# A 3x3 convolution by four outputs from six products down a column, in place of two outputs from four products along a row

## The chip, the cores and the metric

The kernel runs on one core of a Trainium2 chip. The metric is device microseconds of one launch. In the profile PE is TensorE's matmuls, PEld its weight loads, DVE is VectorE, ACT is ScalarE, POOL is GpSimd, and SP is the engine that issues most DMAs. PSUM is the memory into which matmuls write, SBUF the memory that everything else works in, with 128 partitions each.

## What is computed

32 images of 128 channels and 64 x 64 pixels, float32. Each goes through a group norm, a convolution whose weights are mixed for each image, a windowed attention and a scan over its tokens. The part that the change touches is the convolution:

```python
def _L0_conv_ref(x, kernels, fc_w, fc_b):
    pooled = x.mean(axis=(2, 3))
    coeffs = jax.nn.sigmoid(pooled @ fc_w.T + fc_b)
    coeffs = jax.nn.softmax(coeffs, axis=1)
    dyn_k = jnp.einsum('bk,klmij->blmij', coeffs, kernels)
    # one 3x3 convolution for each image, 128 channels in and out, stride 1, padding 1
    ...
x = x + _L0_conv_ref(_gn(x), L0_conv_kernels, L0_conv_fc_w, L0_conv_fc_b)
t = _to_tokens(x)
t = t + _L1_attn_ref(_ln_t(t), ...)
t = t + _L1_ffn_ref(_ln_t(t), L1_ffn_W, L1_ffn_V, L1_ffn_gamma, L1_ffn_beta)
x = _from_tokens(t, x)
```

There are four kernels of 3 x 3 taps to mix, and `_gn` is a group norm with 32 groups of 4 channels. The attention works on windows of 144 tokens with 4 heads of 4 dimensions. The last layer is a scan over the 4096 tokens of an image.

## The kernel before

Channels lie on the partitions. `images()` does everything up to the scan's input, image by image; `by_runs()` (lines 1615 to 1689) then does the scan in runs of 32 tokens with a warm-up of 20. Between them stands only the scan's batch norm.

**Jobs.** The work of an image is cut into generators: `load`, `conv`, `project`, `feed`, `attend`, `divide` (two) and `tail`. They are all put into one list with a place in an order (lines 1139 to 1144): an image's number plus an offset for its stage, `load` at -2.5, `conv` at 0. `conv` also has its first sort key set, so that it comes last of all. A generator yields what its next step needs: an engine, a PSUM tag, the tiles it reads and writes. The loop at lines 1145 to 1162 asks `Clock`, a model of the engines kept while the program is built, when each could go on. It takes the first in the order that could start before the model's TensorE is free, or else the earliest. What a generator issues between two yields goes out as one block. All of this is fixed when the program is built: on the chip each engine runs its own instructions in that order, and waits on semaphores where data or a buffer is not ready. The `Clock` wrapper issues every instruction from line 173, so that the profile gives L173 for nearly everything in `images()`.

**The convolution before.** It uses a minimal filtering scheme along a row: two neighbouring outputs from four products. At the start (lines 364 to 377) the raw taps of the four kernels are loaded, each row's three taps are turned into four (`g4`), and the result is stored to `k_d` in device memory. `load(b)` fetches the image into one of two frames `xs`, with a border of one pixel (66 columns a row), takes its statistics by `bn_stats`, gets the group mean `gm`, writes it into the border, and works out the four coefficients `co`. It then loads `k_d` in eight pieces `kx` (two buffers, 128 x 768) and mixes them into `wb` (lines 581 to 592).

`conv(b)` goes over four blocks of 16 rows. `transform(i)` (line 607) makes the four inputs `ut` of a block, 18 rows of 32 each: three subtractions on POOL and one operation on DVE. Each of the four products is three matmuls of 512 columns, one for each of the kernel's three rows, summed in one PSUM tile `nm`. There are three such tiles, used by all stages. DVE then adds the product to the even or odd columns of the frame, or to both, so the residual is there already.

**Buffers that other stages use.** `places` (line 422) are five SBUF buffers of 1056 elements. `place()` gives one out, and `spare` lists the free ones. `deviations` uses them for squares and statistics. `spread` uses up to three at once for what it loads from device memory: rows of statistics (`r_d`), spread over the partitions, and pieces of the saved image (`x_d`). The attention's score tile `sc` is one PSUM tile of four banks, and POOL makes its masked queries `qe`.

## Time and profile before

| what | value |
|---|---|
| median of three runs | 5544.47 us (5532.93 to 5547.58) |
| the profiled execution's own span | 5544.0 us |
| mean granted TensorE clock | 0.933 of full speed |
| convolution matmuls, records | 3072 of 43571 |
| first and last convolution matmul start | 91.6 and 4661.5 us |
| DMA traffic | 866.15 MB, mean 156 GB/s |
| kx loads | 256 of 384 KB |
| place loads from r_d and x_d | 512 of 512 KB, 128 of 528 KB |

The profile gives for each engine its busy time and its share of the span. A float32 matmul shows as two records, and records overlap, as matmuls are pipelined. "Idle before" is the time for which an engine stood still ahead of a group's instructions, with the instruction that it waited for. The chain is followed back from the last instruction to what released each step, so its shares say who set the end.

The span in 40 slices shows the stages: a start of about two slices, a steady middle, a thin end of `images()` (slices 35 to 37), and the scan. In each string a digit is the busy share in tenths:

```
PE   3898888979989889898898988998988988749995
DVE  5656765666766667676676676666676665448995
ACT  0344333444444344444444444444444444427884
POOL 1331312222322222222222222222222322105774
PEclk9998999989999999999999999999999999869997
```

### The profile page before, as it was taken

The numbers are of one execution on the slowest core, as the hardware profiler recorded it, in microseconds if no ns is written. First come the engines' busy times: TensorE is split into PE (matmuls) and PEld (weight loads), VectorE is DVE, ScalarE is ACT, GpSimd is POOL, SyncE is SP. The second block draws the span as 40 slices with busy tenths as digits, with TensorE's granted clock in tenths as the row PEclk, the third lists the DMA queues.
The fourth block names the chain that finished last, engine by engine and source line by source line (L and its number), as shares of the span: only waits on it lengthen the run. The fifth ranks groups of instructions, "written<-read, shape, count | busy, mean of one in ns | idle before, by whom it ended". The sixth has DMA issues, their size and how long they took to land.

```text
span 5544.0 us, 106009 instructions
## 1 busy us (share of the span) xinstructions
PE 4768.8 (86%) x43571; PEld 2315.6 (42%) x43571; DVE 3648.5 (66%) x5335; ACT 2453.1 (44%) x3852; POOL 1569.2 (28%) x1625
## 2 busy tenths in 40 slices
PE   3898888979989889898898988998988988749995
PEld 1444434444444444444444444444444444314552
DVE  5656765666766667676676666676666765448995
ACT  0344333444444344444444444444444444427884
POOL 1331312222322222222222222222222322105774
PEclk9998999989999999999999999999999999869997
DMA  4515454453445454454454544445545553454997
GB/s 117 153 63 184 129 163 134 141 168 125 154 149 175 138 159 148 144 163 149 142 170 148 164 155 146 160 158 158 158 143 155 159 160 130 136 213 138 269 279 150
DMA packets 456801, 866.15 MB, mean 156 GB/s; under 512 B 297312, under 2 KB 307824, under 8 KB 423536
## 3 DMA queue, kind: packets, MB, share of 16 engines
q1 hardware_dynamic: 447600, 792.12, 44.7%
q0 software_dynamic: 8704, 67.11, 6.0%
q8 instruction: 348, 5.70, 0.4%
q14 instruction: 149, 1.22, 0.1%
HBM read 575.10 MB, written 275.78 MB: 153 GB/s over the span
## 4 chain that ended last, share of the span: by engine, by line
PE 47%; DVE 21%; DMA 14%; ACT 7%; issue 4%; SPq 3%; POOL 2%; DVEq 0%; ACTq 0%; POOLq 0%
PE nm L173 30%; PE sc L173 10%; DVE zt L173 6%; PE av L173 5%; DMA place<-r_d 4%; DVE v L1665 4%; DMA kx<-k_d 3%; ACT ex L173 3%; SPq L173 3%; DMA av<-cd 2%; DVE v L1659 2%; ACT place L173 2%; DVE place L173 2%; DVE frames L173 2%; DVE wb L173 1%
## 5 line engine op out<-in xcount | busy, mean ns | idle before, releaser
L173 ACT ACTIVATE ex<-sc 128x1152 f32<-128x1152 f32 x896 | 1011.6, 1129 | 1303.0 <-PE sc L173 1299.5
L173 PE MATMUL nm<-ut,wb 128*128 128x512 f32 x3072 | 1566.2, 633 | 16.8 <-DVE wb L173 15.6
L173 POOL TENSOR_TENSOR qe<-qs,mqk 128x576 f32<-128x576 f32 x448 | 586.8, 1315 | 1364.1 <-PE sc L173 1332.8
L173 PE MATMUL sc<-qe,ks 32*128 32x288 f32 x7168 | 724.2, 474 | 252.3 <-ACT ext L173 96.8
L173 PEld LDWEIGHTS nm<-ut,wb 128*128 128x128 f32 x3072 | 535.0, 194 | 617.6 <-issue 591.3
L173 POOL TENSOR_TENSOR ut<-frames 128x576 f32<-128x576 f32 x384 | 529.7, 1409 | 865.1 <-PE nm L173 835.8
L173 PE MATMUL av<-ex,VE 128*32 128x144 f32 x14336 | 654.7, 302 | 22.3 <-DVE av L173 21.8
L173 DVE TENSOR_TENSOR frames<-frames,nm 128x512 f32<-128x512 f32 (+1 forms) x640 | 495.1, 791 | 243.3 <-PE nm L173 236.1
L173 PEld LDWEIGHTS sc<-qe,ks 32*128 32x128 f32 x7168 | 296.9, 191 | 807.7 <-issue 270.4
L173 PEld LDWEIGHTS av<-ex,VE 128*32 128x32 f32 x14336 | 372.8, 112 | 354.4 <-issue 263.0
L173 DVE TENSOR_TENSOR zt<-zt,place 128x1024 f32<-128x1024 f32 x256 | 329.2, 1286 | 134.6 <-DMA place<-r_d 109.9
L173 DVE SCALAR_TENSOR_TENSOR wb<-kx,co,wb 128x768 f32<-128x768 f32 x192 | 231.6, 1206 | 217.6 <-DMA kx<-k_d 215.9
L1664 PE MATMUL v<-yw,fVT 128*128 128x256 f32 x1024 | 327.0, 442 | 43.3 <-ACT yw L1668 42.1
L173 ACT ACTIVATE place<-zt 128x1024 f32<-128x1024 f32 x256 | 263.9, 1052 | 189.3 <-DVE zt L173 166.1
L173 PE MATMUL nm<-av,spr 24*32 24x384 f32 (+1 forms) x1280 | 193.2, 600 | 149.9 <-DMA av<-cd 149.7
L173 DVE TENSOR_TENSOR place<-place 128x256 f32<-128x256 f32 x416 | 217.3, 522 | 150.8 <-ACT place L173 141.3
L1669 POOL COPY zr<-yw 128x256 f32<-128x256 f32 x416 | 257.7, 688 | 128.6 <-ACT yw L1668 128.6
L1668 ACT ACTIVATE yw<-v,shf 128x256 f32<-128x256 f32 x512 | 241.6, 473 | 109.2 <-DVE v L1665 74.5
L1665 DVE SCALAR_TENSOR_TENSOR v<-zr,scl,v 128x256 f32<-128x256 f32 x416 | 254.9, 655 | 43.7 <-PE v L1664 43.7
L173 PE MATMUL nm<-place,avg 128*32 128x256 f32 x3072 | 243.1, 396 | 39.4 <-ACT place L173 38.5
L173 ACT COPY zt<-nm 128x512 f32<-128x512 f32 x256 | 148.6, 586 | 264.5 <-PE nm L173 262.2
L173 DVE TENSOR_TENSOR av<-av,nm 128x384 f32<-128x384 f32 (+1 forms) x160 | 89.7, 570 | 260.6 <-PE nm L173 258.2
(191 smaller groups left out, 6006.0 us busy)
## 6 DMA issues: line engine op xcount, KB each, us to landing
place<-r_d SPq DMA_DIRECT2D x512, 512.0 KB
kx<-k_d SPq DMA_DIRECT2D x256, 384.0 KB
x_d<-frames SPq DMA_DIRECT2D x32, 2112.0 KB
place<-x_d SPq DMA_DIRECT2D x128, 528.0 KB
frames<-in_x_dram SPq DMA_DIRECT2D x128, 512.0 KB
out_dram<-zt SPq DMA_DIRECT2D x64, 1024.0 KB
z_d<-zt SPq DMA_DIRECT2D x64, 1024.0 KB
zr<-z_d SPq DMA_DIRECT2D x26, 2048.0 KB
```

The source lines that it names most:

```text
L173: got = f(*args, **kw)
L1659: nc.vector.scalar_tensor_tensor(ps, z, scl, ps, ALU.mult, ALU.add)
L1664: nc.tensor.matmul(ps, fVT, yw[1 - r % 2], start=True, stop=True)
L1665: nc.vector.scalar_tensor_tensor(ps, zt[:, :, :, r], scl, ps, ALU.mult, ALU.add)
L1668: nc.scalar.activation(yw[r % 2], ps, AF.Sigmoid, bias=shf)
L1669: nc.gpsimd.tensor_copy(zt[:, :, :, r], yw[r % 2])
```

## The change

The convolution is done down a column instead: four outputs from six products. `conv` goes over two halves of 32 rows. A half has eight groups of four rows, and each product is three matmuls (one for each of the kernel's three columns) on 8 x 64 = 512 columns. That is 36 matmuls of nm for an image where there were 48.

The tap transform at the start and `k_d` are gone. `load` loads the raw taps of a kernel (128 x 1152) into a place buffer, two ahead, and mixes the four into `h`, whose middle tap gets 1/6 of the identity added: products are multiplied by 6 at the end, and so the residual comes with the convolution. A place buffer grows to 1152 elements. A new job `taps(b)` makes the tap combinations for four of the products (`ws`), three operations on POOL and three on DVE, with waits for the products of the image before that still read them. A new job `waves(b)` makes the six inputs of each half in nine buffers `us` of 8 x 66 elements: seven operations on DVE and five on POOL for each half.

The evacuation of a half is: two products copied from PSUM by ScalarE (`t`), the others combined by ten DVE operations, which write the frame's rows anew. `conv` waits for its waves (`done["wave", ...]`), and writes only when the raw rows have been read (`done["raw", ...]`, `done["edge", ...]`).

```diff
-    k_d = dram.tile([NK, P, 4, 3, P], F32, name="k_d")
...
+    id6 = const.tile([P, P], F32, name="id6")
+    nc.vector.tensor_scalar_mul(id6, ident, 1.0 / 6.0)
...
-    QT, NPL, NF, NZ = T // 4, 5, 2, 3
+    QT, NPL, NF, NZ, NU = T // 4, 5, 2, 3, 9
...
-            with tc.tile_pool(name="gk", bufs=2) as gk:
-                for k in range(NK):
-                    g3 = gk.tile([P, 3, 3, P], F32, name="g3")
-                    nc.sync.dma_start(
-                        g3.rearrange("p i j l -> p (i j) l"), conv_k[:, k].rearrange("m i j l -> m (i j) l")
-                    )
-                    g4 = gk.tile([P, 4, 3, P], F32, name="g4")
-                    nc.vector.tensor_copy(g4[:, 0], g3[:, :, 0])
-                    nc.vector.tensor_copy(g4[:, 3], g3[:, :, 2])
-                    nc.vector.tensor_add(g4[:, 1], g3[:, :, 0], g3[:, :, 2])
-                    nc.vector.tensor_sub(g4[:, 2], g4[:, 1], g3[:, :, 1])
-                    nc.vector.tensor_add(g4[:, 1], g4[:, 1], g3[:, :, 1])
-                    nc.vector.tensor_scalar_mul(g4[:, 1:3], g4[:, 1:3], 0.5)
-                    nc.sync.dma_start(k_d[k], g4)
...
-            places = [kept([P, 16 * (W + 2)], f"place{i}") for i in range(NPL)]
+            places = [kept([P, 9 * P], f"place{i}") for i in range(NPL)]
...
-                ks4 = []
-                def kernel(n):
-                    ks4.append(two.tile([P, 6, P], F32, name="kx"))
-                    nc.sync.dma_start(
-                        ks4[n], k_d[n % NK, :, 2 * (n // NK) : 2 * (n // NK) + 2].rearrange("p j i l -> p (j i) l")
-                    )
-                for k in range(2):
-                    kernel(k)
...
+                gm6 = sml.tile([P, 1], F32, name="gm6")
+                nc.vector.tensor_scalar_mul(gm6, gm, 6.0)
...
+                done["mean", b] = gm, gm6
...
+                taps = []
+
+                def kernel():
+                    w = yield from place("SP", ())
+                    nc.sync.dma_start(w, conv_k[:, len(taps)].rearrange("m i j l -> m (i j l)"))
+                    taps.append(w)
+
+                for k in range(2):
+                    yield from kernel()
                 yield "PE", "nm", (cv,)
                 gv_ps = nm_tile()
                 nc.tensor.matmul(gv_ps[:, 0:1], grp, cv, start=True, stop=True)
...
+                nc.vector.tensor_scalar_mul(gr, gr, 1.0 / 6.0)
...
-                wb = two.tile([P, 12, P], F32, name="wb")
-                for n in range(2 * NK):
-                    if 0 < n < 2 * NK - 1:
-                        yield "SP", "kx", ()
-                        kernel(n + 1)
-                    yield "DVE", None, (co, ks4[n])
-                    k, w = n % NK, wb[:, 6 * (n // NK) : 6 * (n // NK) + 6]
+                h = two.tile([P, 9 * P], F32, name="h")
+                for k in range(NK):
+                    yield "DVE", None, (co, taps[k]), (h,)
                     if k == 0:
-                        nc.vector.tensor_scalar_mul(w, ks4[n], co[:, 0:1])
+                        nc.vector.tensor_scalar_mul(h, taps[k], co[:, 0:1])
                     else:
-                        nc.vector.scalar_tensor_tensor(w, ks4[n], co[:, k : k + 1], w, ALU.mult, ALU.add)
-                done["load", b] = wb, gm2
+                        nc.vector.scalar_tensor_tensor(h, taps[k], co[:, k : k + 1], h, ALU.mult, ALU.add)
+                    spare.append(taps[k])
+                    if k + 2 < NK:
+                        yield from kernel()
+                nc.vector.tensor_add(h[:, 4 * P : 5 * P], h[:, 4 * P : 5 * P], id6)
+                done["load", b] = h
+            ws = [kept([P, 3 * P], f"w{k}") for k in range(4)]
+            def taps(b):
+                while ("load", b) not in done or (b and gone.get(("conv", b - 1), 0) < 8):
+                    yield
+                h = done["load", b]
+                h0, h1, h2 = (h[:, 3 * P * i : 3 * P * (i + 1)] for i in range(3))
+                yield "POOL", None, (h,), (ws[0], ws[1])
+                nc.gpsimd.tensor_add(ws[1], h0, h2)
+                nc.gpsimd.tensor_add(ws[0], ws[1], h1)
+                nc.gpsimd.tensor_sub(ws[1], ws[1], h1)
+                done["taps", b, 0] = h0, ws[0], ws[1]
+                while b and gone.get(("conv", b - 1), 0) < 12:
+                    yield
+                yield "DVE", None, (h,), (ws[2], ws[3])
+                nc.vector.scalar_tensor_tensor(ws[3], h0, 0.25, h2, ALU.mult, ALU.add)
+                nc.vector.scalar_tensor_tensor(ws[2], h1, 0.5, ws[3], ALU.mult, ALU.add)
+                nc.vector.scalar_tensor_tensor(ws[3], h1, -0.5, ws[3], ALU.mult, ALU.add)
+                done["taps", b, 1] = ws[2], ws[3], h2
+            us = [kept([P, 8, W + 2], f"u{k}") for k in range(NU)]
+            def waves(b):
+                while ("mean", b) not in done or (b and ("waves", b - 1) not in done):
+                    yield
+                gx = xs[b % NF]
+                gm, gm6 = done["mean", b]
+                def new(eng, aps):
+                    while not us:
+                        yield
+                    yield eng, None, aps, (us[0],)
+                    while not us:
+                        yield
+                    return us.pop(0)
+                for i in range(2):
+                    d = [gx[:, 32 * i + k : 32 * i + k + 29 : 4, :] for k in range(6)]
+                    f = yield from new("POOL", (gx,))
+                    nc.gpsimd.tensor_sub(f, d[0], d[2])
+                    done["edge", b, i] = True
+                    u2 = yield from new("DVE", (gx,))
+                    nc.vector.scalar_tensor_tensor(u2, d[2], 4.0, d[4], ALU.mult, ALU.subtract)
+                    u3 = yield from new("DVE", (gx,))
+                    nc.vector.scalar_tensor_tensor(u3, d[1], 4.0, d[3], ALU.mult, ALU.subtract)
+                    u1 = yield from new("DVE", (gx,))
+                    nc.vector.scalar_tensor_tensor(u1, u2, gm6, u3, ALU.subtract, ALU.add)
+                    nc.gpsimd.tensor_sub(u2, u2, u3)
+                    done["wave", b, i, 1], done["wave", b, i, 2] = u1, u2
+                    c = yield from new("POOL", (gx,))
+                    nc.gpsimd.tensor_sub(c, d[4], d[2])
+                    nc.vector.scalar_tensor_tensor(f, c, 0.25, f, ALU.mult, ALU.add)
+                    done["wave", b, i, 0] = f
+                    e = yield from new("POOL", (gx,))
+                    nc.gpsimd.tensor_sub(e, d[3], d[1])
+                    g = yield from new("POOL", (gx,))
+                    nc.gpsimd.tensor_sub(g, d[5], d[3])
+                    done["raw", b, i] = True
+                    nc.vector.scalar_tensor_tensor(g, e, -4.0, g, ALU.mult, ALU.add)
+                    done["wave", b, i, 5] = g
+                    nc.vector.scalar_tensor_tensor(u3, e, 2.0, c, ALU.mult, ALU.add)
+                    nc.vector.scalar_tensor_tensor(c, e, -2.0, c, ALU.mult, ALU.add)
+                    done["wave", b, i, 3], done["wave", b, i, 4] = u3, c
+                    us.append(e)
+                done["waves", b] = True
             def conv(b):
-                while ("load", b) not in done or (b and ("conv", b - 1) not in done):
+                while ("taps", b, 0) not in done or (b and ("conv", b - 1) not in done):
                     yield
                 gx = xs[b % NF]
-                def transform(i):
...
-                ut = transform(0)
-                for i in range(4):
-                    nxt = transform(i + 1) if i < 3 else None
-                    xi = rows(gx, 16 * i, 16)
-                    xe, xo = xi[:, :, 0::2], xi[:, :, 1::2]
-                    for k in (0, 3, 1, 2):
-                        yield "PE", "nm", (wb, ut[:, k])
+                gm, gm6 = done["mean", b]
+                for i in range(2):
+                    y = rows(gx, 32 * i, 32).rearrange("p (t j) w -> p t j w", j=4)
+                    y = [y[:, :, j] for j in range(4)]
+                    for n, k in enumerate((1, 2, 0, 5, 3, 4)):
+                        while ("wave", b, i, k) not in done or (k in (5, 3) and ("taps", b, 1) not in done):
+                            yield
+                        u = done["wave", b, i, k]
+                        if k in (0, 1, 2):
+                            w = done["taps", b, 0][k]
+                        else:
+                            w = done["taps", b, 1][k - 3]
+                        yield "PE", "nm", (w, u)
                         ps = nm_tile()
-                        for di in range(3):
+                        for dj in range(3):
                             nc.tensor.matmul(
-                                ps, wb[:, 3 * k + di], ut[:, k, di : di + 16], start=(di == 0), stop=(di == 2)
+                                ps, w[:, P * dj : P * (dj + 1)], u[:, :, dj : dj + W], start=(dj == 0), stop=(dj == 2)
                             )
-                            if di < 2:
+                            if dj < 2:
                                 yield "PE", None, ()
-                        m = ps.rearrange("p (h w) -> p h w", w=W // 2)
-                        if k == 0:
-                            nc.vector.tensor_add(xe, xe, m)
-                        elif k == 3:
-                            nc.vector.tensor_add(xo, xo, m)
-                        elif k == 1:
-                            x2 = xi.rearrange("p h (w o) -> p h w o", o=2)
-                            nc.vector.tensor_add(
-                                x2,
-                                x2,
-                                m.rearrange("p h (w o) -> p h w o", o=1).to_broadcast([P, 16, W // 2, 2]),
-                            )
+                        us.append(u)
+                        gone["conv", b] = 6 * i + n + 1
+                        m = lines(ps)
+                        if k in (1, 3):
+                            t = one.tile([P, BLK], F32, name="tm")
+                            tl = lines(t)
+                            if k == 1:
+                                nc.scalar.activation(t, ps, AF.Identity, bias=gm)
+                            else:
+                                nc.scalar.copy(t, ps)
+                            continue
+                        while ("raw", b, i) not in done or (i == 0 and ("edge", b, 1) not in done):
+                            yield
+                        if k == 2:
+                            nc.vector.tensor_add(y[2], tl, m)
+                            nc.vector.tensor_sub(y[1], tl, m)
+                        elif k == 0:
+                            nc.vector.scalar_tensor_tensor(y[0], m, 6.0, y[2], ALU.mult, ALU.add)
+                        elif k == 5:
+                            nc.vector.scalar_tensor_tensor(y[3], m, 6.0, y[1], ALU.mult, ALU.add)
                         else:
-                            nc.vector.tensor_add(xe, xe, m)
-                            nc.vector.tensor_sub(xo, xo, m)
-                    ut = nxt
+                            nc.vector.tensor_sub(tl, tl, m)
+                            nc.vector.scalar_tensor_tensor(m, m, 2.0, tl, ALU.mult, ALU.add)
+                            nc.vector.tensor_add(y[0], y[0], m)
+                            nc.vector.scalar_tensor_tensor(y[2], m, 4.0, y[2], ALU.mult, ALU.add)
+                            nc.vector.scalar_tensor_tensor(y[1], tl, 2.0, y[1], ALU.mult, ALU.add)
+                            nc.vector.scalar_tensor_tensor(y[3], tl, 8.0, y[3], ALU.mult, ALU.add)
                 done["conv", b] = gx
...
-                    (tail(b), divide(b, 0), divide(b, 1), attend(b), project(b), load(b), conv(b), feed(b))
+                    (tail(b), divide(b, 0), divide(b, 1), attend(b), project(b), load(b), conv(b), feed(b), taps(b), waves(b))
-                    jobs.append([stage == 6, b + (-0.05, -0.15, 0.6, 1.65, -1.25, -2.5, 0, -0.9)[stage], b, g, None])
+                    at = b + (-0.05, -0.15, 0.6, 1.65, -1.25, -2.5, 0, -0.9, -2.4, -2.3)[stage]
+                    jobs.append([stage == 6, at, b, g, None])

```

## What is predicted

> **What bounds the kernel now.** I read the page first (shares, slices, chain, costliest groups), then the groups with shapes kept apart, then the waits, then one tile at a time, then windows and the timeline.
>
> ```profile
> PE 4768.8 (86%) x43571; PEld 2315.6 (42%) x43571; DVE 3648.5 (66%) x5335; ACT 2453.1 (44%) x3852; POOL 1569.2 (28%) x1625
> ...
> PE 47%; DVE 21%; DMA 14%; ACT 7%; issue 4%; SPq 3%; POOL 2%; DVEq 0%; ACTq 0%; POOLq 0%
> PE nm L173 30%; PE sc L173 10%; DVE zt L173 6%; PE av L173 5%; DMA place<-r_d 4%; DVE v L1665 4%; DMA kx<-k_d 3%; ACT ex L173 3%; SPq L173 3%; DMA av<-cd 2%; DVE v L1659 2%; ACT place L173 2%; DVE place L173 2%; DVE frames L173 2%; DVE wb L173 1%
> ...
> L173 PE MATMUL nm<-ut,wb 128*128 128x512 f32 x3072 | 1566.2, 633 | 16.8 <-DVE wb L173 15.6
> ```
>
> TensorE is busiest, the convolution (nm<-ut,wb) is its largest group, and it hardly waits: 16.8 us idle in front of it. But TensorE makes up only 47% of the chain, so a microsecond taken from it is not surely a microsecond gained. In 500 us windows from 500 to 4500 us TensorE is busy 434 to 454, VectorE 314 to 346. The first convolution matmul starts at 91.6 us and the last at 4661.5: 4570/32 = 143 us an image.
>
> **What goes from TensorE.** Four column blocks of 4 products of 3 matmuls (48 an image) become 2 halves of 6 products of 3 (36), all 128x128 on 512 columns. Each shows as two records (3072 = 32 x 48 x 2). The read pattern changes from 512 contiguous elements to 8 rows of 64 at a pitch of 66; nm<-frames,avg reads rows at that pitch at 391 ns against 396 and 413 for contiguous sources, so I charge nothing. Undisturbed speed:
>
> ```profile
> 2121.16 14.86 PE L173 MATMUL nm<-ut,wb 128*128 128x512 f32 x34
> ```
>
> 14.86/34 = 0.437 us a record; 1566.2/3072 = 0.510 with slow-clock stretches and pipeline ends in it. 12 x 2 x 32 = 768 records: 336 or 392 us. If only chain time counts (47% of 86%, a factor 0.55), 336 gives 185. I take 336, because the convolution comes last in the job order and fills whatever is open: bounds 185 and 392.
>
> **What goes at the start.** Four loads of the raw taps, 28 VectorE operations of about 0.55 us (15 us) and four stores to k_d precede the first image's mean (its copy gm runs at 58.2 us, though mv was done at 27.7); POOL's first setup memset waits 50.1 us for k_d<-g. The setup's small SP issues remain. I take 25 us, bounds 0 and 40.
>
> **VectorE, by image.** The rows:
>
> ```profile
> L173 DVE SCALAR_TENSOR_TENSOR ut<-frames,gm x128: 804/1697/1826, 100.4 to 4617.0; 128x576 f32<-128x576 f32 x128
> ...
> L173 DVE SCALAR_TENSOR_TENSOR wb<-kx,co,wb x192: 999/1019/2033, 81.6 to 4540.8; 128x768 f32<-128x768 f32 x192
> ...
> L173 POOL TENSOR_TENSOR ut<-frames x384: 1136/1166/2837, 59.4 to 4616.8; 128x576 f32<-128x576 f32 x192
> ```
>
> (minimum/median/maximum ns). The ut operation on VectorE, issued beside POOL's, takes 804 ns at least and 1697 in the median: it loses about one POOL operation.
>
> Evacuation: before 495.1/32 = 15.5 us (the frames group). After, per half: 4 tensor-tensor from PSUM at 0.685, 4 scalar-tensor-tensor with PSUM at 0.722 (812 ns for 576, times 512/576), 2 from SBUF at 0.99 (between 0.715 and 1.27, scaled from ut's 804 and mean 1427): 7.6, so 15.2. Saves 0.3.
>
> Waves: 14 of 528 elements, 0.737 to 1.308 (ut's minimum and mean, scaled): 10.3 to 18.3, where 180.1/32 = 5.6 stood. I take the upper, since POOL again works on the same image beside it: +12.7 (low +4.7).
>
> Mixing: before (231.6 + 42.8)/32 = 8.6. After one scaling (669 x 1.5 = 1.0), three accumulations (1206 x 1.5 = 1.8) and 0.3 for the identity: 6.7. Saves 1.9. The three operations for ws are new: 3 x 1206/2 = 1.8.
>
> Sum +12.3 us an image (low +4.3), 394 us busy, 73% in all. VectorE is on the chain with 21% for 66% busy, a factor 0.32: +126 us (low 44).
>
> **A rule against it.** The Trainium skill ("SBUF — State Buffer", section "SBUF: two separate sides") says VectorE and GpSimd share a port pair, locked for a whole instruction, by a VectorE operation with two SBUF inputs against a GpSimd one that reads SBUF, and that the loser blocks fully. That speaks against the change, which has 17 such VectorE and 13 GpSimd operations for each image; the ut row above agrees with it. A sum by the rule, each of the 14 waves losing a whole POOL median of 1.166, would be an estimated 14 x (0.737 + 1.166) = 26.6 us in place of 18.3, some 85 us more after the chain's factor.
>
> **ScalarE and POOL.** ScalarE gets 4 copies of 512 from PSUM (zt<-nm, 586 ns): 2.3 us an image, times 7/44, 12 us in all. POOL had 12 x 1.409 = 16.9; it gets 10 x 1.409 x 528/576 and 3 of 384 elements at 0.893 (the kt group): 15.6. Two transforms are issued at once before, six POOL operations (8.68 us at 2184.93 in the timeline) with the attention's qe queued behind; now each waits its own turn. Nothing is taken for it.
>
> **New waits.** In each half VectorE's f waits for POOL's u2 and c, and g for e and its own subtraction: four in-order waits an image of up to 2 x 1.166 = 2.3 us, 9.3 in all. Behind them on VectorE stand the evacuations of nm's three PSUM tiles, for which TensorE waits next. Steps of other jobs can be put in between, so I take half of 9.3 x 0.32 x 32 = 95, that is 48 (bounds 0 and, all of it exposed, 298).
>
> **DMAs and SP's queue.** Eight kx loads of 384 KB (3.07 MB) become four of 576 KB (2.3 MB), issued by SP among the same place and frame loads.
>
> ```profile
> DVE wb L173 <- DMA kx<-k_d: 232.6, 115, 9.3
> ...
> DVE zt L173 <- DMA place<-r_d: 183.7, 77, 8.0
> ```
>
> kx loads are 3% of the chain, 166 us. By count half would go (83), by bytes a quarter (42). But the taps now live in two of the five place buffers, from before the coefficients until they are mixed, and a load waits for a free one behind deviations and spread. I take 20 gained; the bounds are 83 gained and the loss in rival E.
>
> **Sum.** -336 - 25 + 126 + 12 + 48 - 20 = -195 from a span of 5544.0 us (the median is 5544.47, so the two agree): **about 5350 us**. With the high ends of the costs (TensorE 185, start 0, stalls 298, DMA 0) it is 5544 - 185 + 126 + 12 + 298 = 5795; with the low ends 5544 - 392 - 40 + 44 + 12 - 83 = 5085.
>
> **The clock.** Granted clock by stretch:
>
> ```profile
> 2100.00:2150.00 50.00, 49.72 (x326) 24.24 (x328) 36.73 (x43) 13.45 (x23) 11.61 (x12) 1.00 0.66 187
> 2150.00:2200.00 50.00, 42.28 (x546) 21.38 (x534) 32.15 (x51) 26.62 (x37) 19.23 (x17) 0.86 0.34 112
> ```
>
> The columns are TensorE, its weight loads, VectorE, ScalarE and POOL busy, then the clock, the DMA share and GB/s. A full TensorE holds 1.00; where it idles 8 us in 50 the clock is 0.86. Less filler could mean more such stretches. The second rule against the change is in the Trainium skill ("TensorE: Matmul & The Clock Gate", section "Part 1: The HAM clock gate"): an idle window of about 3.4 us halves the clock until TensorE is busy for as long again. By that rule one more slow window an image would be an estimated 1.7 us each, 55 us in all, and 5405 instead of 5350.
>
> **Rivals.**
>
> A, the forecast: most of TensorE's saving arrives, 5350, own range 5190 to 5520. For it: the convolution is active nearly all through the image period and almost never waits. Chance 0.50.
>
> B, all of it arrives and VectorE's additions hide: 5544 - 336 - 25 = 5183. For it, VectorE sits a third of the time; against it, its 21% of the chain. Chance 0.13.
>
> C, nothing gained: filler gone becomes idle time, since the attention's own waits (sc for ex and ext, divide for av<-cd, 149.7 us in 30 waits) set the pace: 5544, within 17 us. Against it, TensorE is busy 90% of the time in mid-run. Chance 0.06.
>
> D, slower, at VectorE's queue: f and g hold VectorE for POOL in every half, TensorE runs out of nm tiles, and all 9.3 us show, together with all of the 12.3 us of added work in place of a third. Then 5544 - 336 - 25 + 298 + 394 + 12 = 5887; with two thirds of both, 5656. It decides from the point where exposed added work passes (336 + 25)/32 = 11.3 us an image, about half of 9.3 + 12.3 = 21.6. For it: a burst of conv alone needs VectorE 7.6 + 9.2 = 16.8 us a half against 36 x 0.437 = 15.7 us of TensorE, where before it was (15.5 + 5.6)/4 = 5.3 against 24 x 0.437 = 10.5. Against it: on average VectorE stays at 73%. Chance 0.24.
>
> E, slower, at the place buffers: with two of five held for some 25 us an image, spread turns its loads over one at a time, 25/5.5 = 4.5 loads (a load of 4.25 us in the chain, 1.28 for its operation) with 4.25 us exposed, 19 us. All exposed: 5350 + 20 + 612 = 5982; with half, 5676. Against it: place waits are 184 us of the whole run now. Chance 0.07.
>
> That the change doesn't do what it says is not likely: the matmul count is in the code.
>
> **How the numbers follow.** A measurement of this kernel tells 0.3% (17 us) from no change. Faster is A and B: 0.63. Same is C: 0.06. Slower is D and E: 0.31. Time 5350; the range, with some 0.1 left out on each side, 5190 to 5680; for the likeliest case alone 5190 to 5520.
>
> **What would show it.** Right: 2304 convolution matmul records near 1175 us busy (1566.2 x 0.75); VectorE at 70 to 76%; TensorE's share in mid-run still above 0.85; waves of 1.1 us or more in the mean; no kx wait, and taps waits under 100 us. Wrong: waits of VectorE for POOL above 300 us (D); place waits well over 184 us (E); TensorE below 0.82 in mid-run or a mean clock under 0.91 (C and the clock); a first convolution matmul not before 85 us (no gain at the start).

## The result, and the profile after

The changed kernel takes **5603.65 us** (median of four, 5598.38 to 5610.41) where the kernel before takes 5546.02 on the same chip: a ratio of 1.0106 (95% interval 1.0091 to 1.0122), 1.1% slower. The forecast was 5350, faster. The time lies inside the range of 5190 to 5680, on the side that had a chance of 0.31.

The first part of the page after (busy time, share of the span of 5603.8 us, instructions), two of its strings of 40 slices, and three of its costliest groups:

```profile
PE 4608.3 (82%) x42803; PEld 2245.8 (40%) x42803; DVE 3894.0 (69%) x5664; ACT 2536.0 (45%) x3980; POOL 1676.5 (30%) x1657
...
PE   4898787888888888797879888888887979648996
...
PEclk9898888989999989898989998999997989769996
...
L173 PE MATMUL sc<-qe,ks 32*128 32x288 f32 x7168 | 781.5, 509 | 296.2 <-ACT ext L173 87.5
L173 PE MATMUL nm<-u,w 128*128 128x512 f32 x1536 | 801.9, 638 | 50.4 <-POOL w L173 34.7
...
L173 PE MATMUL nm<-u,h 128*128 128x512 f32 x768 | 391.8, 622 | 1.9 <-DVE frames L173 1.6
```

The work did what it was to do: 1536 + 768 = 2304 convolution records, 801.9 + 391.8 = 1193.7 us busy, 372.5 less than the 1566.2 of before. But TensorE as a whole lost only 4768.8 - 4608.3 = 160.5 us. The other 212 came back in other groups, at unchanged counts. The score matmuls (sc<-qe,ks) took 724.2 us before, at a mean of 474 ns, and take 781.5 at 509:

```profile
L173 PE MATMUL sc<-qe,ks 32*128 32x288 f32 x7168 | 724.2, 474 | 252.3 <-ACT ext L173 96.8
```

(the kernel before). And TensorE's time without work grew from 5544.0 - 4768.8 = 775 us to 5603.8 - 4608.3 = 995. The mean granted clock fell from 0.933 to 0.89.

One place in TensorE's timeline shows both at once (start, length, engine, tiles, count, and in brackets the idle time before and what ended it):

```profile
2141.24 0.77 PE L173 MATMUL sc<-qe,ks 32*128 32x288 f32 x8 [0.67 <-ACT ex L173]
...
2142.46 0.43 PE L173 MATMUL av<-ext,VT 128*32 128x144 f32 x8
2146.88 0.59 PE L173 MATMUL nm<-mv,grp 128*128 128x1 f32 x2 [3.99 <-DVE mv L173]
2147.39 1.34 PE L173 MATMUL sc<-qe,ks 32*128 32x288 f32 x8
...
2158.29 1.19 PE L173 MATMUL av<-ex,VE 128*32 128x144 f32 x16
...
2162.94 0.77 PE L173 MATMUL sc<-qe,ks 32*128 32x288 f32 x8 [1.23 <-ACT ext L173]
```

The convolution of an image ended at 2132 us and the next began at 2173. In between TensorE has only the attention and the norms. It stands for 3.99 us, and for some 13 us after that the same eight score matmuls take 1.34 us instead of 0.77. The granted clock of this stretch is 0.50, though TensorE is busy for 12.69 of 13 us:

```profile
2147.00:2160.00 13.00, 12.69 (x130) 7.42 (x130) 7.05 (x23) 6.11 (x11) 5.39 (x6) 0.50 0.72 235
```

(length; TensorE, weight loads, VectorE, ScalarE and POOL busy; clock, DMA share, GB/s). Before the change the gaps between one image's convolution and the next were 1 to 28 us for images 8 to 18 (the images ahead of these had gaps of up to 100); after it they are 3 to 103.

VectorE's waits (for what, us in all, times, longest):

```profile
DVE av L173 <- PE nm L173: 213.4, 73, 16.0
DVE av L173 <- PE av L173: 197.3, 80, 12.2
DVE zt L173 <- DMA place<-r_d: 168.9, 64, 14.3
...
DVE u L173 <- POOL u L173: 84.0, 47, 3.8
...
DVE h L173 <- DMA place<-in_conv_k_dram: 27.5, 11, 11.0
```

The 232.6 us for kx have become 27.5 for raw taps. Waits for POOL in the waves are 84.0 us. In VectorE's account (span = busy + not busy) the 5544.0 = 3648.5 + 1895.5 of before have become 5603.8 = 3894.0 + 1709.8: 245.5 us more work, 185.7 less standing, 60 more in all.

### The profile page after: what moved, and what is told of

Read it like the earlier page. It is cut to its first block, busy times and chain, and to the rows that moved or that the text cites. A ratio compares the mean times of both kernels' runs of the same rounds, so it can differ in the third digit from the quotient of the medians.

```text
span 5603.8 us, 104629 instructions
## 1 busy us (share of the span) xinstructions
PE 4608.3 (82%) x42803; PEld 2245.8 (40%) x42803; DVE 3894.0 (69%) x5664; ACT 2536.0 (45%) x3980; POOL 1676.5 (30%) x1657
## 5 line engine op out<-in xcount | busy, mean ns | idle before, releaser
L173 PE MATMUL sc<-qe,ks 32*128 32x288 f32 x7168 | 781.5, 509 | 296.2 <-ACT ext L173 87.5
L173 PE MATMUL nm<-u,w 128*128 128x512 f32 x1536 | 801.9, 638 | 50.4 <-POOL w L173 34.7
L173 POOL TENSOR_TENSOR qe<-qs,mqk 128x576 f32<-128x576 f32 x448 | 616.5, 1381 | 732.9 <-PE sc L173 714.0
L173 PE MATMUL av<-ex,VE 128*32 128x144 f32 x14336 | 696.3, 317 | 37.7 <-DVE av L173 35.7
L173 POOL TENSOR_TENSOR u<-frames 128x528 f32<-128x528 f32 x256 | 390.3, 1537 | 224.4 <-PE nm L173 222.6
L173 PEld LDWEIGHTS nm<-u,w 128*128 128x128 f32 x1536 | 265.7, 195 | 344.0 <-issue 289.0
L173 PE MATMUL nm<-u,h 128*128 128x512 f32 x768 | 391.8, 622 | 1.9 <-DVE frames L173 1.6
L173 POOL COPY xb<-gt 128x896 f32<-128x896 f32 x32 | 30.8, 961 | 1062.5 <-DVE gt L173 1011.9
L173 DVE SCALAR_TENSOR_TENSOR u<-u,u 128x528 f32<-128x528 f32 x256 | 288.0, 1146 | 86.8 <-POOL u L173 84.0
L173 DVE SCALAR_TENSOR_TENSOR zt<-sc,gbc,zt 128x576 f32<-128x576 f32 (+1 forms) x192 | 175.2, 913 | 153.7 <-PE sc L173 153.0
```

Of the source, the lines that this page charges most:

```text
L173: got = f(*args, **kw)
```

## The experiments

Times are medians of two to ten executions; a ratio is to the kernel before on the same chip, with its 95% interval. The kernel before took 5534 to 5546 us on the chips used, and the changed kernel was timed on one of them, so differences to its 5603.65 us hold to about 12 us. Busy times come from the profiled execution. Diffs are excerpts; ... marks a cut.

**The place buffers (rival E).** The taps get two buffers of their own, in eight pieces of half a kernel (HP = 576 elements); the places shrink to their old size, and one wave buffer goes to make room.

```diff
-    QT, NPL, NF, NZ, NU = T // 4, 5, 2, 3, 9
+    QT, NPL, NF, NZ, NU = T // 4, 5, 2, 3, 8
...
-            places = [kept([P, 9 * P], f"place{i}") for i in range(NPL)]
+            places = [kept([P, 16 * (W + 2)], f"place{i}") for i in range(NPL)]
...
-                    w = yield from place("SP", ())
...
+                    yield "SP", "kx", ()
+                    w = two.tile([P, HP], F32, name="kx")
...
```

> The changed kernel with the raw taps in two buffers of their own (half a kernel each, eight loads of 288 KB), place buffers at their old size, and eight wave buffers in place of nine to make room. Theory P (the taps hold two of the five place buffers, so deviations and spread wait, attention starts late and TensorE stands): 100 us or more come back, 5450 to 5510 us. Theory V (VectorE's added work and its waits for POOL set the pace): no change, 5590 to 5630 us.

5650.35 us, 1.0196 (1.0176 to 1.0217). Its control is the changed kernel with eight wave buffers and nothing else:

> The changed kernel with eight wave buffers in place of nine, nothing else: the control for the run with own tap buffers. Both theories: within 20 us of the changed kernel, 5590 to 5625 us.

5550.03 us, 1.0014 (1.0002 to 1.0026). Taking the taps out of the places makes it 100 us slower than the control, where E expects it faster. A surprise stands beside it: fewer buffers made the kernel 54 us faster. The other way round, the kernel before with its kx pieces in place buffers, asked for after the statistics and not ahead of them:

```diff
-                    ks4.append(two.tile([P, 6, P], F32, name="kx"))
+                    w = yield from place("SP", ())
+                    ks4.append(w[:, 0 : 6 * P].rearrange("p (s l) -> p s l", l=P))
...
```

> The kernel before, with only one thing of the change: its eight weight pieces kx go into place buffers, two ahead, asked for at the point where the changed kernel asks for its taps. Theory P: slower than before, 5600 to 5700 us. Theory V: as before, 5530 to 5565 us.

**5478.32 us, 0.9887 (0.9871 to 0.9904): faster than both.** VectorE's wait for the pieces, 232.6 us before and then its largest for a load, became

```profile
DVE wb L173 <- DMA place<-k_d: 76.1, 39, 7.5
```

that is 232.6 - 76.1 = 156 us less waiting for 66 us of time. There is no sign of E's loss of 306 to 612 us in any of the three.

**What the waves cost (rival D).** Constant wave inputs: the 24 operations of an image are left out, on VectorE and POOL, and the convolution reads the buffers as they are.

```diff
-                    f = yield from new("POOL", (gx,))
-                    nc.gpsimd.tensor_sub(f, d[0], d[2])
...
-                    nc.vector.scalar_tensor_tensor(c, e, -2.0, c, ALU.mult, ALU.add)
...
+                    for k in range(6):
+                        done["wave", b, i, k] = us[k]
```

> The changed kernel with the waves left out: the six inputs of each half are constant buffers, so 14 VectorE and 10 POOL operations an image go, and conv waits for no wave (its output is not the reference's). Matmuls, taps and evacuation stay. Theory V: 200 us or more go, below 5400 us. Theory P: the place buffers still hold it up, 5530 to 5600 us.

5294.09 us, 0.9552 (0.9536 to 0.9567): 310 below the changed kernel, and 252 below the kernel before. Its page:

```profile
PE 4468.4 (84%) x42803; PEld 2196.6 (41%) x42803; DVE 3399.6 (64%) x5216; ACT 2535.4 (48%) x3980; POOL 1171.7 (22%) x1346
```

TensorE's records are the same 42803, VectorE's busy time is 494 us lower, POOL's 505. Leaving out one engine's part at a time, first VectorE's 14 operations, then POOL's 10:

> The changed kernel without the 14 VectorE operations of the waves (the wave buffers keep a constant or what POOL writes; the output is not the reference's). POOL's ten stay, and conv waits for them as before. Leaving all waves out gave 5294 us, 310 less than the changed kernel. If VectorE's work is what costs, most of the 310 goes: 5300 to 5400 us. If POOL's work and its share of the port is what costs, little goes: 5500 to 5600 us.

> The changed kernel without the ten POOL operations of the waves (the output is not the reference's). VectorE's 14 stay. If VectorE's work costs: 5500 to 5600 us, though its operations should fall from a mean of 1.0 to about 0.75 us and its waits for POOL go. If POOL's work costs: 5300 to 5400 us.

5346.63 us (0.9654, 0.9625 to 0.9682) and 5361.42 us (0.9680, 0.9633 to 0.9727), two executions each. Their pages, in this order:

```profile
PE 4492.1 (84%) x42803; PEld 2207.8 (41%) x42803; DVE 3541.9 (66%) x5216; ACT 2537.1 (47%) x3980; POOL 1638.2 (31%) x1666
PE 4459.4 (83%) x42803; PEld 2200.8 (41%) x42803; DVE 3749.2 (70%) x5664; ACT 2537.1 (47%) x3980; POOL 1190.0 (22%) x1346
```

VectorE's part is 352 us of its busy time and brings 257; POOL's is 486 us of POOL, with which 145 of VectorE go though it issues the same 5664 operations, and brings 242. The two gains sum to 499 where both together bring 310: they overlap. Next, the waves are made but the convolution's matmuls read a constant tile, so that no product waits for its wave's data:

```diff
-                        u = done["wave", b, i, k]
+                        us.append(done["wave", b, i, k])
+                        u = fWT.rearrange("p (o l) -> p o l", o=1).to_broadcast([P, 4, P])
...
```

> The changed kernel with all waves made, but the matmuls read a constant in their place (the output is not the reference's), so that no matmul stands in wait for a wave, and no wave for a matmul. If the waves cost by the time they take on VectorE and POOL: as the changed kernel, 5560 to 5640 us. If by the waits between them and TensorE: near the run without waves, 5300 to 5400 us.

5550.81 us, 1.0003 (0.9987 to 1.0019): 53 less, little of the 310. So it is not the convolution's wait for the waves that costs most of it. What is left is their work, or what VectorE and POOL wait for inside them.

**In-order waits inside the waves.** Three more points to yield, so that VectorE need not stand behind POOL's subtraction (three added lines like this one):

```diff
+                    yield "DVE", None, (c, f)
                     nc.vector.scalar_tensor_tensor(f, c, 0.25, f, ALU.mult, ALU.add)
...
```

> The changed kernel with three more steps in the waves: u2's subtraction on POOL, and f's and g's operation on VectorE, are each issued in a step of their own once the order model has their inputs ready, so that other work goes in between. Same instructions. Theory H (leaving out either engine's part gave nearly all, so the cost is where the two meet: in-order waits of VectorE for POOL and of POOL for VectorE, and what is queued behind them): 100 us or more less, 5400 to 5500 us. If not the waits but the work costs: 5550 to 5650 us.

5726.26 us, 1.0336 (1.0317 to 1.0354), 122 slower: a miss. All the waves' subtractions on VectorE, none on POOL:

```diff
-                    f = yield from new("POOL", (gx,))
-                    nc.gpsimd.tensor_sub(f, d[0], d[2])
+                    f = yield from new("DVE", (gx,))
+                    nc.vector.tensor_sub(f, d[0], d[2])
...
```

> The changed kernel with the ten POOL operations of the waves moved to VectorE: 24 there an image, none on POOL, so no wait between the two. That is some 10 x 0.7 us more VectorE work an image, 220 us in all, less what the shared port costs now. Theory H: 5400 to 5560 us in spite of it. If VectorE's time is what costs: 5650 us or more.

5566.95 us, 1.0049 (1.0032 to 1.0065): 37 less, with VectorE's busy time up by 96 us to 3990.5 and POOL's down by 491. Ten more operations an image add only 3 us to VectorE. The trace takes part of this apart: the ten take 270.0 us in all, and the 14 others of the waves, which meet fewer of POOL's, fell from 452.4 to 372.6; the rest of the difference lies in other groups.

**TensorE's term.** The kernel before with 36 convolution matmuls an image instead of 48; the third matmul of products 0, 3 and 1 is left out, all else stays:

```diff
-                        for di in range(3):
+                        for di in range(3 if k == 2 else 2):
...
```

> The kernel before with 36 convolution matmuls an image in place of 48: the third matmul of three of the four products is left out (the output is not the reference's); everything else stays. It measures the largest term of the prediction alone. As predicted (TensorE's time counts in full): 336 us less, 5190 to 5240 us. Theory V (TensorE's work is a filler that is not missed, VectorE's queue sets the pace): 5450 to 5560 us.

5588.55 us, **1.0087 (1.0055 to 1.0118)**. Its page, its clock and its convolution:

```profile
PE 4556.6 (82%) x42803; PEld 2265.0 (41%) x42803; DVE 3700.8 (66%) x5335; ACT 2455.3 (44%) x3852; POOL 1572.5 (28%) x1625
...
L173 PE MATMUL nm<-ut,wb 128*128 128x512 f32 x2304 | 1168.5, 632 | 17.0 <-DVE wb L173 11.6
```

The convolution lost 1566.2 - 1168.5 = 398 us, and the time went up by 51. TensorE as a whole lost only 212: the other 186 came back in its other groups, which took longer, at a clock of 0.896, or no longer overlapped the convolution. And it stands for 5580.6 - 4556.6 = 1024 us, 249 more than before. The opposite, the changed kernel with 48 fillers of two small matmuls (128x128 on 128 columns) for each image but one, last in the order like the convolution:

```diff
+            def warm(b):
+                while ("conv", b - 1) not in done or "setup" not in done:
+                    yield
+                for i in range(48):
+                    yield "PE", "nm", ()
+                    t = nm_tile()
+                    for c in range(2):
+                        nc.tensor.matmul(t[:, P * c : P * c + P], fWc, fWc, start=True, stop=True)
...
```

> The changed kernel with work added: a last-ranked job of 48 steps an image of two 128x128 matmuls on 128 columns that nobody reads, some 21 us of TensorE an image. If the lower clock (0.89 against 0.933) is a cause in itself, filling the gaps raises the clock to 0.92 or more and the time stays or falls in spite of the added work: 5480 to 5610 us. If the clock only follows from gaps that other engines make, the added work costs: 5640 to 5900 us.

5709.12 us, 1.0308 (1.0272 to 1.0344), 105 slower, with the clock back at 0.951. In its page, and in its stretch from 2000 to 2500 us:

```profile
PE 5102.5 (89%) x48755; PEld 2884.4 (51%) x48755; DVE 3875.2 (68%) x5664; ACT 2537.6 (45%) x3980; POOL 1676.3 (29%) x1657
...
L173 PE MATMUL nm<-fWc 128*128 128x128 f32 x5952 | 832.2, 290 | 25.0 <-DVE frames L173 9.2
```

```profile
2000.00:2500.00 500.00, 462.38 (x4838) 269.63 (x4830) 330.39 (x470) 214.35 (x316) 130.44 (x110) 0.97 0.45 138
```

In the changed kernel the same stretch reads

```profile
2000.00:2500.00 500.00, 424.35 (x4306) 203.35 (x4302) 350.99 (x476) 221.19 (x322) 145.66 (x114) 0.89 0.44 138
```

So fillers of 832 us, with which TensorE's busy time rises by 494, cost 105, and a clock restored by filler brought no gain that shows. The run adds work and raises the clock together, so it does not give the price of the clock alone.

**VectorE's price.** In the kernel before, the one operation of `transform` on VectorE is issued four times, 384 more in all:

```diff
-                    nc.vector.scalar_tensor_tensor(ut[:, 1], d[1], gm2, d[2], ALU.subtract, ALU.add)
+                    for _ in range(4):
+                        nc.vector.scalar_tensor_tensor(ut[:, 1], d[1], gm2, d[2], ALU.subtract, ALU.add)
```

> The kernel before with VectorE's operation of the transform done four times in place of once: 12 more of 576 elements an image, 0.81 us each alone and 1.43 in the mean beside POOL, so 311 to 548 us more VectorE work. Theory V (about 0.8 us of time for each us of it, as leaving out the waves' ones showed): 5790 to 5980 us. By the factor of the prediction, 0.32: 5645 to 5720 us.

5999.35 us, 1.0811 (1.0766 to 1.0856).

```profile
PE 4768.5 (80%) x43571; PEld 2359.5 (39%) x43571; DVE 4080.4 (68%) x5719; ACT 2453.1 (41%) x3852; POOL 1619.9 (27%) x1625
```

VectorE's busy time is up by 431.9 us, the profiled span by 434 and the median by 462; TensorE's busy time is unchanged. And from the changed kernel, the last four VectorE operations of each half's evacuation left out (the last product is not added to the four rows):

```diff
-                            nc.vector.tensor_add(y[0], y[0], m)
-                            nc.vector.scalar_tensor_tensor(y[2], m, 4.0, y[2], ALU.mult, ALU.add)
-                            nc.vector.scalar_tensor_tensor(y[1], tl, 2.0, y[1], ALU.mult, ALU.add)
-                            nc.vector.scalar_tensor_tensor(y[3], tl, 8.0, y[3], ALU.mult, ALU.add)
```

> The changed kernel without the last four VectorE operations of each half's evacuation (the output is not the reference's): eight an image, 5.8 us, 185 us less VectorE work that has nothing to do with POOL or with a wait for it. Theory V: 5604 less 148, give or take 60 for another order: 5400 to 5515 us. By 0.32: 5545 us, 5485 to 5605.

5446.27 us, 0.9817 (0.9786 to 0.9849).

```profile
PE 4511.2 (83%) x42803; PEld 2210.3 (41%) x42803; DVE 3733.9 (69%) x5408; ACT 2536.0 (47%) x3980; POOL 1669.3 (31%) x1657
```

VectorE's busy time fell from 3894.0 to 3733.9, by 160; the time by 157. That suggested moving VectorE's work to TensorE, which has the room: the taps are mixed by matmuls with diagonal weights, ScalarE makes the diagonals and copies the sums, and the places go back to their old size.

```diff
-                        nc.vector.scalar_tensor_tensor(h, taps[k], co[:, k : k + 1], h, ALU.mult, ALU.add)
...
+                    nc.scalar.activation(dg[:, k], ident, AF.Identity, scale=co[:, k : k + 1])
...
+                        nc.tensor.matmul(ps[:, 0 : 3 * P], dg[:, k], w, start=(k == 0), stop=(k == NK - 1 and i != 1))
...
+                    nc.scalar.copy(h[:, 3 * P * i : 3 * P * (i + 1)], ps[:, 0 : 3 * P])
```

> The changed kernel with the tap mixing moved from VectorE to TensorE: 13 matmuls of 384 columns an image with the coefficients on a diagonal, made and copied out by ScalarE; taps come in six loads of 384 KB through the same place buffers. VectorE loses 180 us, TensorE gains some 0.66 x 13 x 32 = 275 us, ScalarE 75. Theory V: 5604 less 144, give or take 60: 5400 to 5520 us. If TensorE's time counted in full: 5700 us or more.

5686.12 us, 1.0257 (1.0225 to 1.0289): 82 slower than the changed kernel, with VectorE 200 us less busy (3694.4). A miss, and a warning: a microsecond of VectorE is not worth one everywhere. Which of the things added (six loads into places instead of four, 13 matmuls and 7 ScalarE operations in the chain from coefficients to taps) takes it back was not separated.

**The order itself.** The order of instructions is made by a model while the program is built, so every edit also changes the order. `LAG` is that model's time from an end to a start elsewhere, 0.05; it changes nothing but the order, and with it which buffer a job gets. Both kernels at 0.08 and at 0.03:

```diff
-    LAG = 0.05
+    LAG = 0.08
```

> The changed kernel with the order model's lag between engines at 0.08 in place of 0.05: the same instructions in a somewhat other order, to see how much the order alone moves the time. Within 1.5% of 5604 us either way, 5520 to 5690 us, by either theory.

> The kernel before with the same lag of 0.08: the same question for the kernel before. Within 1.5% of 5546 us either way, 5460 to 5630 us, by either theory. If the order alone moves the time as much as the change did (1.1%), the sign of the change is not that of its work.

> The changed kernel with the order model's lag at 0.03: a third order of the same instructions. With 0.05 it took 5604 us, with 0.08 5544. If the order's share in the result is about 1%, it lies anywhere from 5530 to 5660 us; if 5604 is the rule, within 15 us of it.

> The kernel before with the lag at 0.03: its third order. With 0.05 it took 5539 to 5546 us, with 0.08 5571. If the change's own work makes it slower whatever the order, the three pairs differ by 40 to 80 us in the same sense; if not, their signs differ, as they do at 0.05 (+60) and 0.08 (-27).

| LAG | kernel before | changed kernel | difference |
|---|---|---|---|
| 0.03 | 5710.70 (1.0312, 1.0295 to 1.0329) | 5608.06 (1.0123, 1.0104 to 1.0143) | -103 |
| 0.05 | 5546.02 | 5603.65 (1.0106, 1.0091 to 1.0122) | +58 |
| 0.08 | 5570.73 (1.0054, 1.0038 to 1.0070) | 5543.91 (1.0006, 0.9992 to 1.0021) | -27 |

The order alone moves the kernel before over 3% and the changed one over 1%. The measured loss of 1.1% holds for these two programs, but its sign is not settled by what the change computes.

The experiments change the order too. ScalarE runs none of the instructions that the edits of the kernel before touch; yet its sequence departs from that kernel's at the 26th of its 3852 instructions both with 36 matmuls and with the operations added on VectorE, and at the 78th with LAG at 0.08.

Single results that differ by less than the 165 us between the two ends of the middle column can be the order's doing: the 54 of eight buffers, the 100 of the taps' own, the 37 to 157 of the smaller edits, and, though it is the fastest complete version, the 66 of the kx pieces in places. What is too large for that, as far as three orders show: the 310 of the waves and the 257 and 242 of their parts, the 462 of the added operations, of which at least 297 remain (0.69 for each of the 432 us of work), and the 398 us of convolution taken away for no gain. Even if an unlucky order hid 165 us in that run, the gain would be 165 - 51 = 114. It was not timed in other orders.

## Why the prediction was wrong, by its own steps

**TensorE's term is the step that failed.** "I take 336, because the convolution comes last in the job order and fills whatever is open" draws the wrong conclusion from a right observation. Work that fills what is open can be taken away without anything coming earlier. The kernel with 36 matmuls takes this step, with the new order that comes with it: it has 398 us less convolution and is 51 us slower. The lower bound of 185 from the chain's share was too high as well: 114 is the most that the orders seen leave room for. Of the 398 us, 186 came back in TensorE's other groups at the lower clock, and the rest, and more, as standing. This was rival C's mechanism, given 0.06 since TensorE is busy 90% of the time in mid-run: it was busy because the filler was there. With the fillers of small matmuls it is 89% busy again, and the time does not improve. That 5604 still lies between 5190 and 5680 is the width of the range, which covered costs at VectorE and the places, and not this step.

**VectorE's factor of 0.32 was too low.** It was its share of the chain over its share of the span. Added or removed on the spot, VectorE's work counted in full: 432 us of it for 434 in the span (0.69 or more if the order helped), and 160 for 157 (this one a size that the order can make). Left out alone, the waves' 352 us brought 257, a factor of 0.73. The measured total of 245.5 us, at full price, is 246 where 126 were taken. Moving the mixing to TensorE does not fit (200 us less for 82 more), nor does the run with all subtractions on VectorE (96 us more for 37 less); both are sizes that the order can make. So a factor well above 0.32 is shown in one run, full price is argued, and neither is a law.

**The size of VectorE's work** was put too high: 245.5/32 = 7.7 us an image, not 12.3. Waves: 288.0 + 114.2 + 50.2 us in three groups, 14.1 an image (18.3 taken). Evacuation 437.3/32 = 13.7 (15.2 taken), mixing with the identity 182.7/32 = 5.7 (6.7), `ws` 99.0/32 = 3.1 (1.8). The waves by tile (minimum/median/maximum ns):

```profile
L173 POOL TENSOR_TENSOR u<-frames x256: 1298/1318/2428, 33.1 to 4670.0; 128x528 f32<-128x528 f32 x128
L173 DVE SCALAR_TENSOR_TENSOR u<-u,u x256: 692/709/1832, 39.0 to 4674.7; 128x528 f32<-128x528 f32 x128
```

The mean of the second row is 1146 ns, but its median is 709, near its minimum: fewer than half of them are held up. In the trace 129 of these 256 overlap an operation of POOL and take 1583 ns in the mean; the 127 others take 702. In the kernel before 102 of the 128 ut operations overlapped one, at 1584, and the 26 others took 810. So a meeting costs 0.88 us, less than POOL's whole 1.3, and about half of these meet. The Trainium skill's rule on the shared port pair ("SBUF — State Buffer", section "SBUF: two separate sides") fits the long ones, but the estimate made from it, every wave losing a POOL operation, gave 26.6 us an image against 14.1 measured.

**The new waits**, 48 taken: VectorE waits for POOL in the waves for 84.0 us, far under the bound of 298, and under the 300 that were to speak for D. D named the right engine, but through its waits, and 84 us are too few for the 257 that VectorE's part of the waves brings when it is left out. What part POOL's own work has in it stays open: without it the time falls by 242 us, while VectorE's busy time falls by 145.

**The loads**, 20 taken with 83 as the bound: the wait fell by 232.6 - 27.5 = 205 us. Alone, in the kernel before, 156 us less of it came with 66 us of time, which the order could make too. E, the loss at the places, did not come.

**The start**, 25 taken: the first convolution matmul stands at 68.6 us instead of 91.6, 23 earlier and before the 85 that were asked for. (The tap transform had 24 VectorE operations, not 28: six for each of four kernels, 13.1 us in all.) But the last stands at 4728.9 instead of 4661.5, so the image period went from 142.8 to (4728.9 - 68.6)/32 = 145.6 us. That is 32 x 2.8 = 90 us, less the 23 at the start and 8 behind the last convolution: the 60 of the spans.

**The signs.** Right: 2304 records with 1193.7 us (1175 foretold), and waits for taps under 100 us. Missed by little: VectorE at 69% where 70 to 76 were foretold, and waves of 1.01 us in the mean over all 448, where 1.1 or more was (1146 ns is their largest group's). Wrong: TensorE in mid-run was to stay above 0.85; in the eight windows of 500 us from 500 to 4500 us it is at 0.81 to 0.87, 0.84 in the mean. Of C's signs the clock came true, 0.89 where 0.91 was the mark, and TensorE's share in one of the eight windows (0.81 under 0.82). The rule on the clock in the Trainium skill ("TensorE: Matmul & The Clock Gate", section "Part 1: The HAM clock gate") fits the fall: it comes with an idle stretch of about 3.4 us, and the 3.99 us above are one. It does not fit the return, which the page puts after about 3.4 us of sustained work: here the clock stays at 0.50 for some 13 us with TensorE busy. That the estimate made from the rule was too small (55 us) can be seen from the 212 us that TensorE's other groups gained in busy time; what this costs in time was not measured alone.

Put together by what the runs measured, TensorE 0, VectorE +246 at full price, the start -23 and the loads between -66 and -205, with ScalarE and the waits left out, the sum lies between 18 and 157 us above the kernel before; 58 was measured. This agrees, and proves little: the order alone can move the time by more.

## What to carry to other kernels

That an engine is busiest, and that its largest group never waits, does not give that group's time a price: leave a part of it out of the kernel before, alone, and see whether the time follows, before costing a change that removes it. The work that came last in the order here filled the time in which other engines were waited for, and taking it away left the waits. Where a list scheduler fixes the order while the program is built, compare both kernels under two or three orders before a per cent is called the change's.

## What the runs showed of the hardware that was not expected

POOL's subtraction takes longer for fewer elements: 528 in 8 rows of 66 take 1298 ns at least and 1318 in the median, where 576 in 18 rows of 32 took 1136 and 1166. The two also read at different steps, but that is not the reason, since the subtractions that read whole buffers take as long; the reason stays open:

```profile
L173 POOL TENSOR_TENSOR u<-u,u x64: 1295/1312/2432, 36.4 to 4623.3; 128x528 f32<-128x528 f32 x64
```

VectorE's operations with one source in PSUM keep their time beside POOL's:

```profile
L173 DVE SCALAR_TENSOR_TENSOR frames<-nm,frames x192: 627/683/694, 79.9 to 4731.6; 128x512 f32<-128x512 f32 x192
```

Of these 192, 73 overlap an operation of POOL and take 683 ns in the mean; the 119 others take 684. The waves that read SBUF alone range from 691 to 1832.

TensorE, busy for 12.69 of 13 us after a stop of 3.99, was granted half its clock for all of them. These are mostly small matmuls with 32 rows or columns of weights, and whether that is why was not tested.
